# Two accumulator banks for the last sequence's second mixture, its halves normalised and stored apart, and a new order of issue

## The chip, the core and the metric

The kernel runs on one core of a Trainium2 chip. The metric is device time in microseconds (us) of one execution. Beside three timed executions there is one profiled execution, whose trace gives a start and a duration for every instruction.

The engines are called as the profile calls them: PE (matrix multiplication; PEld is its weight load, which runs beside it), DVE (vector engine), ACT (scalar engine), POOL (GpSimd) and SP, whose queue issues nearly all the transfers between the DRAM and the on-chip memory. PE writes into PSUM, which has 8 banks; one bank holds 128 x 512 numbers of 4 bytes.

## The reference

The input x is 8 sequences of 512 tokens of 128 features. Four stages follow one another, each of the form `x = layernorm(x + stage(x))`:

1. an encoder with linear attention (16 heads of 64, feature maps with a random projection, the keys' maximum over the whole data) and a feed-forward part of 512 hidden units,
2. a mixture of 8 experts of 64 hidden units, the two best per token ("first mixture"),
3. softmax attention with 16 heads and rotary positions,
4. a mixture of 8 experts of 176 hidden units, the two best per token, and one more expert that every token passes ("second mixture").

The change touches the fourth stage:

```
scores = softmax(xf @ gate_w.T)
_, idx = top_k(scores + gate_b, 2)
w      = take_along_axis(scores, idx)            # rw: (tokens, 8), zero elsewhere
h      = silu((xf @ w1 + b1) * (xf @ w3 + b3))   # for each expert
oe     = h @ w2 + b2
y      = einsum('te,ted->td', rw, oe)
z      = the shared expert, in the same form
x      = layernorm(x + y + z)
```

The layernorm has no gain and no bias here: `(x - mean) / sqrt(var + 1e-5)`, over 128 features.

## The kernel before

**Tiling.** P = 128, a sequence is NT = 4 tiles of 128 tokens. Every operation is first recorded as a "work" (one instruction, or a few that stay together). The function `issue` then issues the 4883 works in the order of a written-out list, `ORDER` (from L129). A second list, `BANK_OF`, gives every PSUM tile its bank, one digit each. Both lists were worked out by a planner beforehand. Each engine runs its own works in the order of the list; between engines there are only the semaphores that the data and the reuse of buffers and banks ask for. So the list decides what stands ahead of what in each engine's queue, and the stages of different sequences lie interleaved.

**The second mixture** is done in two ways. The tokens of sequences 0 to 5 are sorted by expert: POOL scatters them with indirect DMAs (L1664), the experts' tiles are worked through (weights fetched L1696, results stored L1703), and `combine` brings every sequence's tokens back: `xs`, the mixture's input with the shared expert, is loaded (L1853) into a buffer that all sequences share, eight indirect DMAs of POOL gather the results (L1672), DVE adds them with their gates (L1859), a layernorm follows, and SP stores the sequence (L1863). Sequences 6 and 7 go through `dense_mixture` (from L1497), with every expert for every token: at the end of the kernel the combines of sequences 4 and 5 lie beside the dense mixture of sequence 7, and that of 6 ends there as well.

**`dense_mixture`** first runs the router and turns its gates over by transposes (L1507, copied to the DRAM at L1510). The hidden units come in FC2 = 13 chunks of 128. One chunk takes
- a transfer that spreads the gates' rows over partitions (L1050),
- the products with W1 (L1521) and W3 (L1522) into a slot of two PSUM banks,
- ACT's copy of the first with its bias (L1524), after which the first bank is free,
- DVE's product of it with the second bank plus bias (L1526), after which the second bank is free,
- ACT's tanh (L1529), the multiplication with the gates' rows (L1531, on POOL for sequence 7 and on DVE for sequence 6), and DVE's last step of the silu (L1532),
- two chunks later, the product with W2 for the four token tiles (L1547), which adds into one bank `yp` over all the chunks.

PE does each float32 product in two passes, so a chunk's L1547 shows as x8.

After the last chunk DVE adds the residual to the 512 columns of `yp` (L1553), `layernorm` normalises the four tiles, and one transfer of 256 KB stores the sequence (L1555).

**`layernorm`** (L1024, with `moments`, L1010) takes four bn_stats (L1014) and four bn_aggr (L1016) on DVE, one addition of epsilon for the four tiles (L1018), one power of -1/2 on POOL (L1020), one multiplication on DVE for the shift (L1027) and four scalings on ACT (L1029). Its small buffers come from rings of two places for each name, shared by the layernorms of one lane, here "m"; the statistics' buffer has one place. So the power of a layernorm waits for the last scaling of the layernorm two before it, which reads the buffer that the power writes.

**The end.** After the last work SP and POOL read a flag (L1925) that would send the kernel into another form of the attention, and the program's end (L2019) drains every engine.

Of the kernel before, what the change touches and what calls it, by code (L numbers as in the profile page):

```python
# [31 lines left out]
ALU = mybir.AluOpType  # L32
# [3 lines left out]
P = 128  # L36
B, N, D = 8, 512, 128
# [92 lines left out]
    1319, 858, 983, 859, 1320, 984, 1313, 862, 985, 989, 860, 1321, 1316, 863, 861, 990, 864, 1001, 991, 865, 1317,  # L130
    866, 992, 867, 998, 868, 1318, 993, 1335, 869, 1334, 1322, 1000, 870, 1323, 628, 994, 880, 1324, 881, 1331,
    1325, 995, 1314, 999, 886, 1336, 1330, 883, 884, 1003, 1332, 1002, 1004, 887, 1005, 1350, 1333, 1351, 1006,
    882, 1010, 1009, 1337, 889, 1338, 1007, 1008, 890, 1352, 1011, 681, 888, 1370, 1012, 885, 1339, 1015, 1326,
    1020, 891, 1017, 1340, 1353, 1016, 1025, 1022, 892, 1021, 1327, 1018, 1030, 1013, 1341, 893, 1328, 1342, 1023,
    894, 1329, 1032, 895, 1027, 1019, 896, 1024, 898, 1026, 897, 899, 900, 901, 1346, 902, 904, 1343, 1031, 903,
    1371, 1028, 905, 1344, 906, 1345, 1372, 1029, 1300, 907, 1033, 911, 1354, 1014, 908, 1373, 909, 1034, 910,
    1046, 1133, 1035, 1355, 1134, 1039, 1037, 1347, 1038, 1036, 1041, 1042, 1043, 1040, 1050, 1135, 1044, 1049,
    1045, 1048, 1047, 1356, 1137, 1147, 1138, 1136, 1348, 1139, 1148, 1051, 1141, 1149, 1055, 1365, 1059, 1053,
    1151, 1374, 1057, 1366, 1054, 1052, 1375, 1061, 1367, 1058, 1056, 1062, 1060, 1063, 1711, 1357, 1140, 1064,
    1368, 1150, 1142, 1358, 1714, 1152, 1349, 1359, 1395, 1715, 1065, 1143, 1069, 1360, 1068, 1369, 1145, 1376,  # L140
    1067, 1066, 912, 1716, 682, 1070, 1396, 1399, 1400, 1153, 1071, 1144, 1361, 1091, 1240, 1095, 1146, 1717, 1093,
    1154, 1092, 1097, 1096, 1072, 1094, 1156, 1155, 1098, 1362, 1073, 1729, 1099, 1377, 1074, 1363, 1075, 1378,
    1718, 1076, 1364, 1730, 1157, 1077, 1078, 1158, 1385, 1079, 1082, 1386, 1080, 1083, 1174, 1719, 1081, 1379,
    1084, 1085, 1086, 1087, 1387, 1720, 1380, 1088, 1731, 1388, 1089, 1090, 1175, 1159, 1100, 1389, 1397, 1106,
    1160, 1721, 1381, 1101, 1161, 1162, 1382, 1383, 1712, 1722, 1163, 1165, 1103, 1164, 1107, 1384, 1166, 1723,
    1102, 1390, 1167, 1110, 1391, 1169, 1724, 1109, 1168, 1104, 1392, 2110, 1170, 1173, 1193, 1171, 1108, 1393,
    1172, 1179, 1394, 1111, 1176, 1398, 1402, 1733, 1105, 1178, 1401, 1403, 1732, 1404, 1112, 1177, 1405, 1113,
    1725, 1406, 1407, 1408, 1114, 1726, 1409, 1727, 1728, 1115, 1180, 1116, 1183, 1182, 1119, 1120, 1117, 1410,
    1123, 1181, 1118, 1124, 1122, 1734, 1121, 1125, 1126, 1411, 1184, 1735, 1187, 1412, 1185, 1414, 1186, 1736,
    1127, 1737, 1413, 1419, 1129, 1131, 1128, 1191, 1130, 1415, 1532, 1416, 1188, 1533, 1215, 1421, 1536, 1192,  # L150
    1420, 1546, 1189, 1422, 1417, 1534, 1537, 1547, 1538, 1418, 1190, 1535, 1540, 1429, 1548, 1424, 1539, 1431,
    1550, 1197, 1426, 1549, 1425, 1541, 1749, 1198, 1738, 1427, 1423, 1551, 1194, 1430, 1750, 1542, 1195, 1432,
    1543, 1199, 1751, 1428, 1200, 1552, 1196, 1545, 1445, 1745, 1201, 1744, 1713, 1752, 1433, 1214, 1746, 1739,
    1132, 1205, 1434, 1436, 1202, 1437, 1435, 1770, 1438, 1203, 1440, 1442, 1439, 1441, 1443, 1446, 1444, 1769,
    1447, 1204, 1740, 1553, 1771, 1206, 1209, 1207, 1772, 1555, 1753, 1208, 1554, 1450, 1544, 1448, 1451, 1210,
    1452, 1449, 1754, 1212, 1453, 1454, 1456, 1455, 1213, 1457, 1211, 1755, 1216, 1556, 1458, 1459, 1741, 1219,
    1461, 1460, 1218, 1462, 1742, 1463, 1747, 1217, 1557, 1464, 1756, 1757, 1468, 1466, 1465, 1220, 1748, 1467,
    1223, 1221, 1471, 1222, 1224, 1225, 1227, 1226, 1228, 1229, 1231, 1230, 1558, 1559, 1232, 1560, 1561, 1233,
    1562, 1794, 1564, 1743, 1563, 1565, 1472, 1234, 1566, 1473, 1568, 1235, 1798, 1236, 1567, 1569, 1237, 1758,
    1591, 1572, 1573, 1238, 1759, 1574, 1571, 1239, 1570, 1764, 1241, 1765, 1774, 1244, 1766, 1242, 1245, 1243,  # L160
    1773, 1257, 1248, 1258, 1760, 1575, 2111, 1578, 1592, 1576, 1249, 1246, 1247, 1250, 1775, 1251, 1577, 1259,
    1776, 1252, 1777, 1582, 1254, 1253, 1256, 1579, 1761, 1778, 1762, 2115, 1763, 1255, 1779, 2114, 1580, 1767,
    2116, 1581, 1639, 1784, 1768, 1785, 1780, 1583, 1786, 1586, 1781, 1782, 2112, 1585, 1783, 1787, 2510, 1584,
    1789, 1788, 1790, 1795, 1796, 2117, 1587, 1791, 1590, 1613, 1800, 1588, 1614, 1792, 1589, 1593, 1793, 2113,
    1596, 1797, 1595, 1799, 1801, 1802, 1803, 2118, 1594, 1804, 2119, 1597, 1806, 1808, 1601, 1805, 2120, 1807,
    1602, 1809, 2121, 1604, 2122, 1810, 1603, 1598, 1813, 1599, 2123, 1600, 1818, 1814, 2124, 1605, 1815, 1608,
    1820, 1819, 1823, 1607, 1816, 1811, 1817, 1606, 1821, 1812, 1828, 1824, 2125, 1825, 1822, 1298, 1830, 1609,
    1829, 1612, 1826, 1610, 1831, 1827, 1844, 1611, 1832, 2126, 2127, 1615, 1833, 2130, 1617, 1834, 1836, 1837,
    2129, 1835, 1616, 1840, 1839, 1838, 1846, 1618, 1847, 2131, 1841, 1842, 2128, 1843, 1622, 1851, 1619, 1845,
    2133, 1848, 1620, 1850, 1849, 1855, 2134, 1859, 1621, 1852, 1853, 1856, 2132, 2145, 2144, 2150, 1860, 2146,  # L170
    1854, 1857, 1858, 1861, 2149, 2135, 1862, 2154, 2151, 2136, 2137, 2153, 1626, 1863, 2138, 2155, 1623, 1866,
    2139, 2152, 2147, 1624, 1625, 1260, 2156, 1867, 2148, 1474, 1630, 2194, 1261, 2157, 1627, 2140, 1262, 1628,
    1864, 2141, 1299, 1263, 1629, 1264, 1265, 2158, 1266, 1267, 2198, 2142, 1268, 2143, 1469, 2159, 1301, 1631,
    1470, 2165, 1303, 2164, 1632, 1494, 2166, 1302, 1475, 2160, 1304, 1492, 1865, 1476, 1477, 1495, 1490, 1481,
    1478, 1633, 1479, 1491, 1496, 1480, 1482, 2167, 1493, 1634, 1483, 1497, 1484, 1635, 1498, 2169, 1485, 1486,
    1305, 1487, 2170, 1488, 1269, 2161, 1306, 1489, 2162, 2168, 1307, 2163, 1308, 1499, 1309, 1271, 1636, 1500,
    2171, 1310, 1699, 2174, 1503, 1272, 1637, 1270, 2173, 2195, 2172, 1638, 2511, 1502, 1273, 2184, 1640, 1506,
    2185, 1501, 1505, 2186, 1644, 1509, 2518, 1656, 1641, 1643, 1508, 1647, 1642, 2514, 1646, 1311, 1645, 1504,
    2187, 2175, 1870, 1648, 1274, 1507, 2515, 1649, 1510, 1650, 2516, 2199, 2188, 1511, 1657, 1275, 1871, 1651,
    1872, 1658, 1654, 1512, 1284, 2517, 1655, 1653, 1652, 1513, 2176, 1286, 2177, 1697, 1514, 2196, 2178, 1276,  # L180
    1515, 1659, 2179, 2519, 1517, 1660, 1518, 1521, 1519, 1278, 1516, 1698, 1522, 2520, 1523, 1520, 1279, 2521,
    1280, 1524, 2180, 1525, 1661, 1700, 2522, 1868, 1526, 2181, 1662, 1529, 1701, 2512, 1869, 3675, 2182, 1281,
    1530, 1282, 1889, 1702, 1527, 1528, 1283, 1663, 1285, 1895, 2200, 1664, 2523, 2038, 1531, 1890, 1931, 1703,
    1676, 1891, 1896, 1873, 1932, 2183, 1893, 2524, 1935, 1892, 1894, 1933, 1936, 1665, 1874, 1937, 1704, 1945,
    1939, 2529, 1875, 1934, 1946, 1876, 1897, 1705, 2525, 1706, 1707, 1880, 2534, 1938, 1948, 1708, 1940, 2190,
    1877, 1709, 2533, 1947, 1710, 2189, 3275, 1878, 1941, 2530, 1949, 2191, 1881, 1943, 1666, 2549, 1287, 2535,
    1879, 2531, 1942, 2192, 1882, 2532, 2098, 1944, 1950, 2550, 1883, 2513, 2193, 1884, 2197, 1885, 2536, 2201,
    1886, 1951, 2551, 1667, 2202, 1952, 1953, 1887, 2552, 2570, 1888, 2203, 1954, 1668, 2569, 1670, 2204, 1669,
    2208, 1671, 2206, 1288, 1672, 1292, 2205, 1673, 2207, 1899, 2537, 2209, 1898, 1294, 1956, 2210, 1674, 2526,
# [399 lines left out]
def kernel(ctx: ExitStack, tc: tile.TileContext, i: dict, out: bass.AP):  # L589
# [418 lines left out]

    def moments(lane, src, eps):

        st = tiny(lane, [P, NT, 6], "ln_st", 1)
        mv = tiny(lane, [P, NT, 2], "ln_mv")
        for t in range(NT):
            nc.vector.bn_stats(st[:, t, :], src[:, t, :])  # L1014
# [1008 lines left out]
```

## Time and profile before

| | us |
|---|---|
| median of three executions | 1111.16 |
| their range | 1108.29 to 1113.31 |
| profiled execution | 1104.42 |
| its span, first to last instruction | 1102.3 |
| PE, from its last matmul to the end of the span | 12.6 |

The profiled execution took 2.1 us more than its span and 6.7 us less than the median.

In the trace's lines the columns are: start and duration in us, engine, line of the code, operation, result <- operands (names of buffers), shape, and the count of instructions that the line puts together. A bracket holds the idle time of the engine just before them and the instruction that ended it. A line whose engine ends in q (SPq, POOLq) belongs to the engine's queue: issue of a transfer, waits, drains. In the table by stretches each row has, for each engine, its busy time with the count of instructions, then the clock granted to PE (1.00 is full speed), the share of the DMA engines' time, and the GB/s that they moved.

### The profile page before, as it was taken

How to read it: one execution, taken by the hardware profiler on the slowest of the kernel's cores; microseconds unless marked ns; L12 is line 12 of the kernel's file. 1: busy time of each engine (PE TensorE's matmuls, PEld its weight loads, DVE VectorE, ACT ScalarE, POOL GpSimd, SP SyncE). 2: the span in 40 equal slices, each digit the busy share in tenths (PEclk: the TensorE clock that was granted, in tenths of full speed). 3: DMA queues.
4: the chain of work that ended last, by engine and by line, in shares of the span. 5: the costliest groups of instructions: out<-in, count | busy, mean ns of one | idle time of the engine just before them, and what ended most of it. 6: DMA issues, size and time to landing. Idle time of an engine off the chain costs nothing. (4 is left out here: it accounts for less than half of the span.)

```text
span 1102.3 us, 16710 instructions
## 1 busy us (share of the span) xinstructions
PE 1027.1 (93%) x5689; PEld 579.1 (53%) x5689; DVE 816.3 (74%) x1929; ACT 714.8 (65%) x971; POOL 432.9 (39%) x386
## 2 busy tenths in 40 slices
PE   7999999998989999998999999999899988889995
PEld 4444444576564535565545545545587646453563
DVE  4865665788897756899776887877689865765875
ACT  3343545556646788756788687898666675778644
POOL 1222235123363523426763162554324402516363
PEclk9999999999999999999999999999999999889998
DMA  7027430353405132014332222331367866662542
GB/s 213 1 74 255 122 120 2 104 186 140 123 33 193 48 136 87 2 58 154 124 123 79 87 98 90 99 117 64 115 181 226 257 192 179 196 179 82 141 129 72
DMA packets 103372, 134.53 MB, mean 122 GB/s; under 512 B 19650, under 2 KB 60669, under 8 KB 103281
## 3 DMA queue, kind: packets, MB, share of 16 engines
q1 hardware_dynamic: 99905, 126.55, 36.5%
q0 software_dynamic: 3072, 6.30, 2.0%
q8 instruction: 47, 0.77, 0.3%
q10 hardware_dynamic: 304, 0.56, 0.1%
q14 instruction: 44, 0.36, 0.1%
HBM read 81.93 MB, written 54.43 MB: 124 GB/s over the span
## 5 line engine op out<-in xcount | busy, mean ns | idle before, releaser
L1338 ACT ACTIVATE scratch<-ps 128x1024 f32<-128x1024 f32 x256 | 248.7, 1027 | 63.6 <-PE ps L1332 54.9
L1344 PE MATMUL ps<-scratch,vv 128*32 128x512 f32 x1024 | 141.1, 608 | 1.9 <-ACT scratch L1338 1.0
L1089 POOL TENSOR_TENSOR scratch<-scratch 128x1024 f32<-128x1024 f32 x32 | 67.9, 2122 | 121.9 <-ACT scratch L1086 84.5
L1332 PE MATMUL ps<-qx,kx 32*128 32x512 f32 x512 | 72.6, 500 | 9.6 <-ACT scratch L1338 4.3
L826 ACT ACTIVATE scratch<-ps 128x1024 f32<-128x1024 f32 x32 | 32.3, 1020 | 64.5 <-PE ps L821 64.5
L1332 PEld LDWEIGHTS ps<-qx,kx 32*128 32x128 f32 x512 | 28.4, 183 | 85.0 <-ACT scratch L1338 31.2
L1113 PEld LDWEIGHTS ps<-scratch 128*128 128x128 f32 x512 | 60.6, 192 | 17.3 <-issue 7.4
L1065 PE MATMUL ps<-wq,scratch 128*128 128x512 f32 x128 | 65.8, 621 | 3.7 <-ACT scratch L1070 1.2
L1113 PE MATMUL ps<-scratch 128*128 128x128 f32 x512 | 64.1, 278 | 2.1 <-ACT scratch L1109 1.2
L1075 PE MATMUL ps<-wqf,scratch 128*128 128x512 f32 x128 | 64.2, 605 | 1.7 <-DMA scratch<-xT_d 1.5
L1664 POOL DMA_INDIRECT x_d<-scratch,slots x48 | 52.8, 1100 | 29.0 <-DVE m_base L1734 12.8
L860 PE MATMUL ps<-scratch,x_sb 128*128 128x512 f32 x128 | 62.6, 598 | 0.6 <-DVE scratch L837 0.5
L821 PE MATMUL ps<-scratch 128*128 128x512 f32 x128 | 62.7, 618 | 0.4 <-ACT scratch L813 0.4
L1672 POOL DMA_INDIRECT scratch<-x_d,slots x48 | 48.5, 1010 | 34.8 <-DVE m_ln_st L1014 13.5
L831 PE MATMUL ps<-scratch 128*128 128x512 f32 x128 | 60.9, 598 | 0.0
L1832 PE MATMUL ps<-scratch 128*128 128x256 f32 (+1 forms) x252 | 55.1, 357 | 5.3 <-DMA scratch<-w_d 4.5
L828 DVE TENSOR_REDUCE scratch<-scratch 128x16 f32<-128x1024 f32 x32 | 38.4, 1210 | 26.0 <-ACT scratch L826 26.0
L1020 POOL TENSOR_TENSOR f_ln_rs<-f_ln_ve,nhalf 128x4 f32<-128x4 f32 x24 | 26.4, 1100 | 76.0 <-DVE f_ln_ve L1018 74.5
L869 POOL TENSOR_TENSOR scratch<-scratch 128x1024 f32<-128x1024 f32 x7 | 16.5, 2357 | 94.5 <-ACT scratch L855 77.5
L1832 PEld LDWEIGHTS ps<-scratch 128*128 128x128 f32 x252 | 41.6, 199 | 14.6 <-ACT scratch L1338 4.3
L1344 PEld LDWEIGHTS ps<-scratch,vv 128*32 128x32 f32 x1024 | 22.6, 108 | 48.7 <-issue 37.2
L1070 ACT ACTIVATE scratch<-ps 128x1024 f32<-128x1024 f32 x32 | 32.8, 1023 | 22.4 <-PE ps L1065 19.8
(293 smaller groups left out, 2456.9 us busy)
## 6 DMA issues: line engine op xcount, KB each, us to landing
halves_d<-scratch SPq DMA_DIRECT2D x32, 512.0 KB
scratch<-w_d SPq DMA_DIRECT2D x42, 386.0 KB
x_d<-scratch SPq DMA_DIRECT2D x27, 512.0 KB
scratch<-g_d SPq DMA_DIRECT2D x68, 128.0 KB
kx<-halves_d SPq DMA_DIRECT2D x32, 256.0 KB
qx<-halves_d SPq DMA_DIRECT2D x32, 256.0 KB
scratch<-z_d SPq DMA_DIRECT2D x8, 520.0 KB
kvo_d<-scratch SPq DMA_DIRECT2D x8, 512.0 KB
```

Of the source, the lines that this page charges most:

```text
L821: nc.tensor.matmul(kp_ps[:, a, :], xT[:, t * P : (t + 1) * P], wk[:, a * 512 : (a + 1) * 512], start=True, stop=True,)
L831: nc.tensor.matmul(dp_ps[:, a, :], xT[:, t * P : (t + 1) * P], wkf[:, a * 512 : (a + 1) * 512], start=True, stop=True,)
L860: nc.tensor.matmul(xp_ps[:, a, :], x_of(b)[:, t, :], ek[:, t, a * 512 : (a + 1) * 512], start=(t == 0), stop=(t == NT - 1),)
L1065: nc.tensor.matmul(qp[:, a, :], xT[:, t * P : (t + 1) * P], wq[:, a * 512 : (a + 1) * 512], start=True, stop=True,)
L1075: nc.tensor.matmul(dp[:, a, :], xT[:, t * P : (t + 1) * P], wqf[:, a * 512 : (a + 1) * 512], start=True, stop=True,)
L1089: nc.gpsimd.tensor_tensor(pr, eq, zr[:, 0:HM], ALU.mult)
L1113: nc.tensor.matmul(at_ps[:, 0:D], qnT[:, c, :], kvo[:, c, :], start=(c == 0), stop=(c == 7))
L1332: nc.tensor.matmul(halves[g // 2][:, g % 2, :], kx[quarter, kt * P : (kt + 1) * P], qx[quarter, :], start=True, stop=True, tile_position=( ...
L1338: nc.scalar.activation(pr[:, 2 * a : 2 * a + 2], sc, AF.Exp, scale=1.0 / math.sqrt(HD2))
L1344: nc.tensor.matmul(av[32 * g : 32 * g + 32, :], vv[:, head_columns(4 * g + j, kt, j % 2)], pr[:, g, :], start=(j % 2 == 0 and kt == 0), st ...
L1664: inst = tc.nc.gpsimd.indirect_dma_start(out=rows_d, out_offset=bass.IndirectOffsetOnAxis(ap=slots_, axis=0), in_=tokens_, in_offset=None)
L1832: nc.tensor.matmul(to, w[:, c : c + P], xf, start=True, stop=True)
```

## The change

For sequence 7, the last, the second mixture gets two accumulator banks: the W2 products of token tiles 0 and 1 add into one and those of tiles 2 and 3 into the other, over all the chunks. The last chunk's products are issued as two groups, one for each bank. After them come, for each half, an addition of 256 columns, a layernorm of two tiles and a store of 128 KB. `moments` and `layernorm` take the count of tiles from their argument. Sequence 6, and the form that the flag would bring, keep one bank.

```
     def moments(lane, src, eps):
-        st = tiny(lane, [P, NT, 6], "ln_st", 1)
-        mv = tiny(lane, [P, NT, 2], "ln_mv")
-        for t in range(NT):
+        nt = src.shape[1]
+        st = tiny(lane, [P, NT, 6], "ln_st", 1)[:, 0:nt]
+        mv = tiny(lane, [P, NT, 2], "ln_mv")[:, 0:nt]
+        for t in range(nt):
             nc.vector.bn_stats(st[:, t, :], src[:, t, :])
...
-        nc.gpsimd.tensor_tensor(rs, ve, nhalf[:, 0:NT], ALU.pow)
+        rs = tiny(lane, [P, NT], "ln_rs")[:, 0:nt]
+        nc.gpsimd.tensor_tensor(rs, ve, nhalf[:, 0:nt], ALU.pow)
...
     def dense_mixture(xb, dst, gate=nc.vector):
...
-        yp = psb("yp", brief=False)
+        halves_of = [range(NT)] if gate is nc.vector else [range(0, NT // 2), range(NT // 2, NT)]
+        yps = [psb("yp", brief=False) for _ in halves_of]
...
-                with nc.together():
-                    for t in range(NT):
-                        nc.tensor.matmul(
-                            yp[:, t * D : (t + 1) * D], ahead[n - 2][:, t * P : (t + 1) * P],
-                            fw2[:, turns[n - 2], :],
-                            start=(n == 2 and t == 0), stop=(n == FC2 + 1 and t == NT - 1),
-                        )
+                parts = halves_of if n > FC2 else [range(NT)]
+                for ts in parts:
+                    with nc.together():
+                        for t in ts:
+                            nc.tensor.matmul(
+                                yps[t * len(yps) // NT][:, t * D : (t + 1) * D],
+                                ahead[n - 2][:, t * P : (t + 1) * P], fw2[:, turns[n - 2], :],
+                                start=(n == 2 and t % len(halves_of[0]) == 0),
+                                stop=(n == FC2 + 1 and (t + 1) % len(halves_of[0]) == 0),
+                            )
         res = tile2("m_res")
-        nc.vector.tensor_tensor(tok(res), tok(yp), xb, ALU.add)
-        layernorm("m", tok(res), tok(res), 1e-5)
-        nc.sync.dma_start(dst, tok(res))
+        for ts in parts:
+            some = slice(ts[0], ts[-1] + 1)
+            now = tok(res)[:, some]
+            nc.vector.tensor_tensor(now, tok(yps[ts[0] * len(yps) // NT])[:, some], xb[:, some], ALU.add)
+            layernorm("m", now, now, 1e-5)
+            nc.sync.dma_start(dst[:, some], now)
```

`ORDER` and `BANK_OF` are made anew, with 4889 works and one bank digit more. The six new works are a group of PE (the last chunk's products come as two groups of the same matmuls), three of DVE (a second addition L1553, a second L1018, a second L1027), a second power of POOL and a second store of SP; the counts of bn_stats, bn_aggr and ACT's scalings stay.

The first 943 works, up to about 281 us in the profiled execution, are in the same order as before. After that works have changed places with their neighbours on each engine:

| engine | works moved | of | largest shift, places |
|---|---|---|---|
| PE | 132 | 1227 | 6 |
| DVE | 536 | 1900 | 12 |
| ACT | 177 | 905 | 5 |
| POOL | 90 | 329 | 9 |
| SP | 166 | 501 | 13 |

33 of the 880 other PSUM tiles have another bank. For the last 45 us this means: the two accumulators hold banks 7 and 5 from the first W2 products of sequence 7 to their additions, and the two-bank slots of its chunks, which were the pairs from banks 0, 2 and 4 in turn, are the pairs from 0 and 2 alone.

Near the end the order is changed in these places. POOL issues all eight gathers of sequence 5 (L1672) ahead of the power of sequence 4's combine (L1020); before, seven stood ahead of it. In ACT's queue the first scaling of sequence 4's layernorm (L1029) stands ahead of a tanh (L1529) and of the bias copy of the next chunk (L1524). At the very end SP's stores come in the order: sequence 5, first half of 7, sequence 6, second half of 7. ACT's last scalings are those of sequence 6, 5 and 7 mixed, with the two pairs of sequence 7's halves last but for one of sequence 6 between them.

## The prediction on record

> **What bounds the kernel.** I read the page's shares first, then the table by stretches, then the timeline of the last 40 us.
>
> ```profile
> span 1102.3 us, 16710 instructions
> PE 1027.1 (93%) x5689; PEld 579.1 (53%) x5689; DVE 816.3 (74%) x1929; ACT 714.8 (65%) x971; POOL 432.9 (39%) x386
> ```
>
> PE is busy for 1027.1 of 1102.3 us. Of the 75.2 us in which it is not, 5.7 lie before the first matmul and 12.6 after the last (1088.58 + 1.16 = 1089.74 below), so some 57 us of idle time are spread over the whole. The change leaves PE's matmuls as they are, so it can gain in the 12.6 and 57 us only. By stretches:
>
> ```profile
> 1050.00:1090.00 40.00, 38.63 (x190) 24.56 (x189) 32.85 (x90) 18.00 (x32) 25.18 (x22) 1.00 0.36 102
> 1090.00:1102.30 12.30, 0.00 (x0) 0.00 (x0) 2.14 (x12) 4.59 (x12) 1.42 (x2) 0.67 0.25 70
> ```
>
> Where the accumulators are split, PE (first column after the length) is idle for 1.4 of 40 us. Then comes a tail without PE. In the timeline it reads:
>
> ```profile
> 1088.58 1.16 PE L1547 MATMUL ps<-scratch 128*128 128x128 f32 x8 [0.26 <-DVE scratch L1532]
> ...
> 1089.77 0.69 DVE L1553 TENSOR_TENSOR scratch<-ps,scratch 128x512 f32<-128x512 f32 x1 [0.15 <-PE ps L1547]
> ...
> 1092.42 1.01 POOL L1020 TENSOR_TENSOR m_ln_rs<-m_ln_ve,nhalf 128x4 f32<-128x4 f32 x1 [2.01 <-ACT scratch L1029]
> ...
> 1093.66 1.65 ACT L1029 ACTIVATE scratch<-scratch,m_ln_nm,m_ln_rs 128x128 f32<-128x128 f32 x4 [0.22 <-DVE m_ln_nm L1027]
> ...
> 1095.33 0.37 SPq L1555 DMA_DIRECT2D out_dram<-scratch  x1
> ```
>
> Addition, statistics, power, four scalings, store. The end itself is in the instructions of line 2019, by queue (durations in ns, least/median/most, then first and last start):
>
> ```profile
> L2019 POOLq DRAIN  x3: 40/107/7905, 1093.5 to 1102.0; - x3
> L2019 SPq DRAIN  x3: 7/7/13, 1099.5 to 1101.7; - x3
> ```
>
> SP, after the last store, drains at 1099.5. POOL's drain begins at 1093.5, right after its last power (1092.42 + 1.01), and takes 7.9 us, to 1101.4; the span ends 0.9 later. So **POOL's last power sets the end, 8.9 us after it; the last store has 1.9 us of slack** (1101.4 - 1099.5). Whether that drain is a fixed length after the power or waits for something else, this trace does not show; I keep both.
>
> **The change part by part.**
>
> *The end.* The last group of matmuls, 1.16 us, becomes two; the first half is complete some 0.5 earlier. Additions: 0.69 us for 512 columns, 0.34 us for 128; by the line between them 256 columns take 0.46, so the second half's addition ends at 1089.77 + 0.46 or, if it waits for the first, later by little. Statistics and scalings keep their counts (four bn_stats at 0.28, four bn_aggr, four L1029 at 0.4 to 0.48). Added on DVE's path are one L1018 and one L1027 (0.17 and 0.16), and a power on POOL. A power of two columns is not in the trace: it lies between 0.56 (eight rows, one column, L905) and 1.01 (four columns); I take 0.75. Both powers wait for rings: the first for the scalings of sequence 5, which have tiles 0 and 1 done by about 1091.5; it then runs to 1092.3. The second waits for its L1018 (about 1092.5, two statistics of the second half and the second small add behind the first half's) and ends between 1093.1 and 1093.7 instead of 1093.43. By POOL's drain the end moves by **-0.3 to +0.3; I take +0.1**, as two serial powers cost what the split wins. If the stores set the end instead, the last two scalings end at about 1094.95 instead of 1095.31 and the store is half as large: **-0.6 to -1.0**. Both ends are kept.
>
> At the trace's rows the halving of work per instruction is dear: 0.46 x 2 = 0.92 for 0.69 us of addition. [...]
>
> *The second bank* costs no instruction, but takes bank 5 from the slots of sequence 7's chunks: two slots instead of three. A slot is held from W1 to the end of L1526: two products of 0.86 us and a response, from W3's end to L1526's end, that was 0.85 to 1.9 us in this stretch but for one case. PE takes 2.6 us for a chunk, so two slots come round in 5.2 us and cover a response up to 2.6. The one case is here:
>
> ```profile
> 1062.78 1.05 POOL L1020 TENSOR_TENSOR m_ln_rs<-m_ln_ve,nhalf 128x4 f32<-128x4 f32 x1
> ...
> 1064.06 1.26 ACT L1029 ACTIVATE scratch<-scratch,m_ln_nm,m_ln_rs 128x128 f32<-128x128 f32 x3 [1.80 <-DVE m_ln_nm L1027]
> ...
> 1065.22 1.88 PE L1522 MATMUL ps<-scratch 128*128 128x512 f32 x4
> ...
> 1065.22 0.67 ACT L1524 ACTIVATE scratch<-ps,cols 128x512 f32<-128x512 f32 x1
> ...
> 1065.93 0.75 DVE L1526 SCALAR_TENSOR_TENSOR scratch<-ps,cols,scratch 128x512 f32<-128x512 f32 x1 [1.91 <-ACT scratch L1524]
> ```
>
> The bias copy waits behind three scalings of sequence 4's combine, which waited for its power. L1526 ends at 1066.68, 3.9 us after its matmuls. Before, the next products (second half of the x4 row, 1066.08) had a third slot. With two they go into this one: a stall of 1066.68 - 1066.08 = **0.6 us**. Besides, POOL now has one more gather (1.03 to 1.3 us with its issue) ahead of that power, and ACT a scaling ahead of a tanh and of this bias copy: the chain comes 1.3 us later, the stall is **1.9**. Against that, the planner's shifts may let the bias copy pass in time: 0. I take **1.3**, between the two stalls, as both moves are certain from the order and only their overlap with slack is not.
>
> *What then comes later.* Sequence 4's store waits for its scalings, and its buffer's next load for the store:
>
> ```profile
> 1066.82 0.41 SPq L1863 DMA_DIRECT2D out_dram<-scratch  x1
> ...
> 1070.58 0.34 SPq L1853 DMA_DIRECT2D scratch<-xs_d  x1
> ```
>
> The load came 3.8 us after the store and takes 4.5 us to land (the row of 1046.07). Later by 1.2 to 2.5, it delays the additions of sequence 5 (L1859, first at 1075.82), which stand in DVE's one queue ahead of L1526 and L1532 of two chunks; DVE is 82% busy here (32.85 of 40) and has little to give back. With that the last matmul comes up to **3.1** us later (1.9 and half of 2.5). If PE's slack of 1.4 us takes the delay up, nothing of it is left.
>
> *The rest of the order.* PE has 132 of 1227 works moved, by six places at most, DVE 536 of 1900. No instruction is added before 1050 us. The moves that looked dangerous are covered: a power moved behind six scatters (869) has them ready 10 us earlier, in a hole of POOL from 860 to 869; a result store (L1703) moved ahead by 13 places was ready long before. So I cost the rest at nothing. Its cover is those 57 us of idle time; about a tenth of PE's works have moved, and a tenth of 57 us is **6 us either way**, an estimate that serves as spread.
>
> **The sum.** End +0.1, stall and its consequences +1.3, rest 0: +1.4 on the profiled execution, 1104.4 -> 1105.8, and put on the median of the runs, 1111.16 -> **1112.6**. 0.5%, or 5.6 us, is about what a measurement of this kernel can tell from no change.
>
> **Rivals.**
> - *Two slots bind* (slower, 0.25). The stall at 1065 delays sequence 4's store, sequence 5's load and its additions, and each of the last chunks finds its slot held. For it: DVE at 82%, one queue for both. Against: all but one response fit into 2.6 us. It decides once two chunks in a row answer later than 2.6 us. +3.1, and with two more stalls of 1.9 up to +7: 1114.3 to 1118.2.
> - *The split does its work* (0.15). The drain follows the stores, or the early first half brings the second power forward, and the slots cost nothing: -1.0, with the gaps of 1.1 us before it closed as well -2.1: 1109 to 1110.2; with luck in the order down to 1105.
> - *It does not do what it says* (0.15). The stores' gain lies under POOL's drain, nothing is won at the end, and the reordering from 281 us on decides, by the spread of 6: 1105 or 1117. I lean to the slower side of it (0.09 to 0.06), since an engine that is 93% busy has less to win than to lose.
>
> **Chances and range.** The forecast gets 0.45 and stays within 0.5% (1105.6 to 1116.7), as do half of the first rival (0.12) and three quarters of the second (0.11): 0.68 together. Faster by more: 0.04 of the second and 0.06 of the third, 0.10. Slower by more: 0.13 of the first and 0.09 of the third, 0.22. The range goes from the third's lower end, 1105, to the first's upper end, 1118.2; it is wide because of the order, not of the split.
>
> **What would show it.** The forecast: in the changed trace a gap of PE of 0.6 to 2 us before an L1522 or L1521 near 1066, released by DVE's L1526; sequence 4's store about 1 us later; POOL's drain beginning at 1093 to 1095 and again near 8 us long; SP's drain well before its end. If the drain shrinks as the power moves, the end hangs on something else, and the second rival is right. Gaps of PE at every second chunk after 1070 would show the first. If the time before 1050 us differs by more than 2 us, the order has decided, and I was wrong to cost it at nothing. An added wait to see: the first power behind the scalings of sequence 5 (POOL's idle time before it released by ACT).

## The result and the profile after

| | us |
|---|---|
| median of seven executions before | 1111.16 (1107.31 to 1114.9) |
| median of seven executions after | 1121.22 (1116.92 to 1125.03) |
| profiled execution after, its span | 1120.62, 1118.9 |

The ratio is 1.0091, with a 95% interval of 1.0065 to 1.0117: slower by 10 us, above the upper end of the forecast range (1118.2).

The page of the profile after begins:

```profile
span 1118.9 us, 16724 instructions
PE 1032.4 (92%) x5689; PEld 585.3 (52%) x5689; DVE 813.1 (73%) x1932; ACT 714.3 (64%) x971; POOL 431.9 (39%) x387
```

PE's busy time is 5.3 us longer for the same 5689 matmuls (the mean granted clock of this execution was 0.981, and 0.987 before), and its idle time between the first and the last matmul is 68 us, where it was 57. The first 280 us agree within 0.1 us. The place of the predicted steps, the timeline of the last 40 us after (start, duration, engine, line; all lines have moved on by 2 to 10):

```profile
1078.54 1.04 POOL L1021 TENSOR_TENSOR m_ln_rs<-m_ln_ve,nhalf 128x4 f32<-128x4 f32 x1
...
1081.43 0.75 DVE L1530 SCALAR_TENSOR_TENSOR scratch<-ps,cols,scratch 128x512 f32<-128x512 f32 x1 [1.66 <-ACT scratch L1528]
...
1082.24 1.12 PE L1526 MATMUL ps<-scratch 128*128 128x512 f32 x2 [1.15 <-DVE scratch L1530]
...
1103.30 1.16 PE L1553 MATMUL ps<-scratch 128*128 128x128 f32 x8 [0.42 <-DVE scratch L1536]
...
1104.98 1.16 PE L1553 MATMUL ps<-scratch 128*128 128x128 f32 x8 [0.52 <-DVE scratch L1536]
```

This is the predicted stall: the W3 product waits 1.15 us for DVE's product to free one of the two slots, behind the power of sequence 4's combine. The last two groups wait 0.42 and 0.52 us, where only one waited 0.26. In the last 48 us before the last matmul's end PE is idle for 2.09 us after and 1.10 before. The end:

```profile
1105.90 0.42 DVE L1563 TENSOR_TENSOR scratch<-ps,scratch 128x256 f32<-128x256 f32 x1
...
1108.00 0.70 POOL L1021 TENSOR_TENSOR m_ln_rs<-m_ln_ve,nhalf 128x2 f32<-128x2 f32 x1 [1.24 <-DVE scratch L1563]
...
1109.00 0.69 POOL L1021 TENSOR_TENSOR m_ln_rs<-m_ln_ve,nhalf 128x2 f32<-128x2 f32 x1 [0.30 <-DVE m_ln_nm L1029]
```

Its drains, from the instructions of the program's end (ns; first and last start):

```profile
L2029 POOLq DRAIN  x3: 40/107/7905, 1109.8 to 1118.6; - x3
L2029 SPq DRAIN  x3: 7/7/13, 1115.3 to 1118.3; - x3
```

From PE's last matmul to the end it is 12.7 us after, 12.5 before (by the matmul's recorded end). So the last 60 us are as forecast, and some 15 us between the two profiled executions, 8 to 9 between the medians, came from 281 to 1040 us, where the forecast had put nothing. The largest single gap of PE there reads as follows in the timeline after:

```profile
1029.45 0.94 POOL L1682 DMA_INDIRECT scratch<-x_d,slots  x1 [0.30 <-issue]
...
1029.46 0.50 PE L1334 MATMUL ps<-qx,kx 32*128 32x512 f32 x4 [1.11 <-issue]
...
1034.90 1.94 ACT L1340 ACTIVATE scratch<-ps 128x1024 f32<-128x1024 f32 x2 [4.98 <-remote]
...
1036.89 0.80 PE L1334 MATMUL ps<-qx,kx 32*128 32x512 f32 x4 [4.85 <-ACT scratch L1340]
```

ACT's exponential reads the four products that PE issued at 1029.46 and that end by their model at 1029.96. ACT starts at 1034.90, released by no instruction that the trace knows ("remote"). In the trace's record of the semaphore, PE's own update, the signal that these products are done, is dated 4.9 us after their end. As that end is modelled, the trace can't tell a signal that came late from products that themselves ended late; in what follows "late" covers both. PE meanwhile issued what else it could, then waited for ACT. Comparing every update of PE's semaphore with the end of the last matmul ahead of it, I call a signal **late** when more than 0.3 us lie between. Up to 1070 us the sum of late stretches is 12.8 us in the trace before and 16.3 after. In both, every one over 0.5 us lies within 0.6 us of an issue of POOL's indirect DMAs; all the time so close to an issue is 14% of the span. ACT, DVE and POOL have no late signal before the program's end. Behind the stall the granted clock was halved for 6.8 us. In the table by stretches after (PE busy is the first number after the length, the clock the third from the end):

```profile
1020.00:1045.00 25.00, 18.16 (x119) 8.57 (x118) 10.88 (x31) 14.98 (x21) 8.79 (x9) 0.86 0.38 100
```

### The profile page after: what moved, and what is told of

Read it like the earlier page. It is cut to its first block, busy times and chain, and to the rows that moved or that the text cites. A ratio compares the mean times of both kernels' runs of the same rounds, so it can differ in the third digit from the quotient of the medians.

```text
span 1118.9 us, 16724 instructions
## 1 busy us (share of the span) xinstructions
PE 1032.4 (92%) x5689; PEld 585.3 (52%) x5689; DVE 813.1 (73%) x1932; ACT 714.3 (64%) x971; POOL 431.9 (39%) x387
## 5 line engine op out<-in xcount | busy, mean ns | idle before, releaser
L1340 ACT ACTIVATE scratch<-ps 128x1024 f32<-128x1024 f32 x256 | 249.2, 1027 | 74.1 <-PE ps L1334 54.5
L826 ACT ACTIVATE scratch<-ps 128x1024 f32<-128x1024 f32 x32 | 32.3, 1020 | 64.5 <-PE ps L821 64.5
L1674 POOL DMA_INDIRECT x_d<-scratch,slots x48 | 50.5, 1052 | 29.8 <-DVE m_base L1744 12.7
L1093 DVE TENSOR_REDUCE f_den<-scratch 128x16 f32<-128x1024 f32 x32 | 38.7, 1209 | 15.5 <-POOL scratch L1091 15.4
L1726 ACT ACTIVATE scratch<-scratch 128x512 f32<-128x512 f32 (+2 forms) x48 | 29.3, 614 | 30.9 <-DVE scratch L1722 16.6
```

The costliest lines, as they stand in the source:

```text
L1340: nc.scalar.activation(pr[:, 2 * a : 2 * a + 2], sc, AF.Exp, scale=1.0 / math.sqrt(HD2))
L1674: inst = tc.nc.gpsimd.indirect_dma_start(out=rows_d, out_offset=bass.IndirectOffsetOnAxis(ap=slots_, axis=0), in_=tokens_, in_offset=None)
```

## The experiments

Theory at first: the new order of the middle costs the time, the split what the prediction gave it. Rival: the second bank and the two slots cost it. In the edits, "order" stands for `ORDER` and `BANK_OF` together.

**1. The split with the old order, the new order without the split, and halves of it.** All four on one chip, on which before took 1094.44 us.

```
 split, old order       after.py:   order of before up to its 4600th work (1043 us), then the changed one
 new order, one bank    before.py:  changed order up to its 4600th work, then that of before
 first part             before.py:  changed order up to its 2867th work (700 us), then that of before
 second part            before.py:  changed order from the 2867th to the 4600th work
```

> The changed code with its two accumulators, its two slots and its own order for the last 60 us, but with the order and the banks of before up to about 1043 us. Theory 1 (the new order of the middle costs the time, the split only what the prediction gave it): +1 to +3 us, ratio 1.001 to 1.003. Theory 2 (the second bank and the two slots cost the time): +8 to +10 us, ratio 1.007 to 1.009.

> The code of before with one accumulator, one addition and one store, with the changed order and banks up to about 1043 us and the order of before for the last 60 us. Theory 1: +7 to +9 us, ratio 1.006 to 1.008. Theory 2: between -1.5 and +1.5 us.

> The code of before with the changed order and banks only up to about 700 us, the order of before from there on. Theory 1: by the lag of the two profiled executions at 700 us (3.7 us of 16) about a fourth of the loss, +2 to +4 us. Theory 2: between -1.5 and +1.5 us.

> The code of before with the changed order and banks only from about 700 to 1043 us. Theory 1: the rest of the loss, +5 to +7 us, so that this and the run with the first part add up to the run with both. Theory 2: between -1.5 and +1.5 us.

| | ratio to before | interval |
|---|---|---|
| split, old order | 1.0025 | 1.0005 to 1.0044 |
| new order to 1043 us, one bank | 0.9985 | 0.9965 to 1.0005 |
| first part | 0.9988 | 0.9966 to 1.0010 |
| second part | 0.9994 | 0.9970 to 1.0018 |

The split's +2.7 us fits both forecast and theory 1; the order costs nothing, against theory 1, which gave +7 to +9 us for it. Neither theory gives the 10 us. Part of the +2.7 us is probably not the split's own: in that trace PE also waits 1.86 us at the router's transposes of sequence 7 (L1509), just behind the place where the two orders join. There it waits 0.30 us in the trace before and not at all in that of the changed kernel. And before itself was 17 us quicker than in the first measurement. None of the four traces has a late signal.

**2. The changed kernel again, all of it but the split, and the last power left out.** A second such chip (before 1095.73).

```
 everything but the split   before.py with the changed order and banks throughout
```

```
-        nc.gpsimd.tensor_tensor(rs, ve, nhalf[:, 0:NT], ALU.pow)
+        nc.gpsimd.tensor_tensor(rs, ve, nhalf[:, 0:NT], ALU.pow) if power else nc.vector.tensor_copy(rs, ve)
...
-        layernorm("m", tok(res), tok(res), 1e-5)
+        layernorm("m", tok(res), tok(res), 1e-5, gate is nc.vector)
```

> The changed kernel itself, again, beside the kernel before. The parts measured so far (order of the middle -1.6 us, split with its end +2.7 us) add up to +1.1 us, not to the +10.1 us of the first measurement. If the parts simply add up, +0 to +3 us (ratio 1.000 to 1.003). If the parts hurt only together (order of the middle and the split), +8 to +12 us (1.007 to 1.011) wherever it is measured.

> The code of before, one accumulator, one addition and one store, but with the whole changed order and the changed banks, so also two slots instead of three for the last chunks and the changed queues of the last 60 us. If the slots and queues of the end make the loss of the split variant (+2.7 us), this stands 1 to 2 us above the run with the new order up to 1043 us (-1.6 us): -0.5 to +1 us, with a gap of PE of 0.6 to 1.9 us behind DVE's product of the chunk at the combine of sequence 4. If the halved normalisation makes it, -1.6 us and no such gap.

> The code and order of before; for the last sequence alone the power is left out and DVE copies the variance into its place, so its scalings use a wrong factor. If POOL's last power sets the end by its 7.9 us drain, POOL's last power is then the one of the layernorm before it, which ends 3.0 us earlier, and the time from the last matmul to the end of the span falls from 12.6 to some 9.5 to 10.0 us, the stores taking over. If the stores or something else set it, it falls by no more than the 0.9 us that the copy is shorter, to 11.7 or more, and POOL's drain changes its length.

The changed kernel: 0.9991 (0.9959 to 1.0022), so no loss. All but the split: 0.9983 (0.9955 to 1.0010), -1.9 us; with an interval from -4.9 to +1.1 us that can't decide between the two times expected of it, though the wait that was expected with the slots is there (0.90 us, below). The same place as above in this trace of the changed kernel:

```profile
1011.28 0.94 POOL L1682 DMA_INDIRECT scratch<-x_d,slots  x1 [0.31 <-issue]
...
1011.28 0.50 PE L1334 MATMUL ps<-qx,kx 32*128 32x512 f32 x4 [1.11 <-ACT scratch L1340]
...
1011.89 1.94 ACT L1340 ACTIVATE scratch<-ps 128x1024 f32<-128x1024 f32 x2
```

The same gather beside the same products; ACT starts 0.11 us after their end and does not wait. The stall of the two slots is there as well: 1.11 us in the changed kernel, 0.90 with one bank and the changed order, 1.22 in the split with the old order, and in none of the kernels with three slots. The end takes 13.4 us with the changed order and one bank, 12.7 with the split: the halves win back 0.7 us that their own order loses.

Without the last power the drains are:

```profile
L2019 POOLq DRAIN  x3: 40/107/7905, 1081.8 to 1091.7; - x3
L2019 SPq DRAIN  x3: 7/7/13, 1091.1 to 1091.4; - x3
```

POOL's drain has the same 7905 ns and begins behind what is now POOL's last power; it is over at 1089.7, and SP, with the stores, now comes last (1091.1). From the last matmul to the end it is 11.0 us instead of 12.5. I expected 9.5 to 10: the mechanism holds, the stores took 1 us more than I gave them.

**3. Where the loss comes back.** New theory A: the loss belongs to chips on which PE's signals come late. Rival B: it is in the order, and was missed by chance.

> The changed kernel a third time, to see on which chip it loses. In the first measurement (+10.1 us) the traces of both kernels hold signals of PE that come up to 4.9 us late, and before took 1111 us; on two other chips there were none, before took 1094 to 1096 us, and this kernel was not slower. Theory A (the loss belongs to a chip on which PE's signals come late): +8 to +12 us where before takes about 1111 us and the trace shows late signals, -3 to +3 us where before takes about 1095 us and it shows none. Theory B (the loss is in the order, and the second measurement missed it by chance): +5 us or more here, whatever the time of before.

> The code of before with the changed order and banks up to about 1043 us, again. Theory A: -2 to +1 us on a chip without late signals; on one with them most of the loss of the changed kernel, +6 to +10 us, as the late signals of its trace lie at 545 to 1035 us. Theory B: +4 us or more on any chip.

> The changed code with the order and banks of before up to about 1043 us, again. By the profiles its last 48 us hold 2 us of idle PE instead of 1, and the end is 0 to 0.2 us longer: +1 to +3 us on any chip, by both theories.

These three, unchanged from parts 1 and 2, fell on a third chip, where before took 1111.02 us:

| | ratio to before | interval |
|---|---|---|
| changed kernel | 1.0082 | 1.0051 to 1.0112 |
| new order to 1043 us, one bank | 1.0060 | 1.0029 to 1.0090 |
| split, old order | 1.0011 | 0.9982 to 1.0041 |

All three traces have late signals: 17.4, 19.6 and 15.8 us in sum. It went as theory A said, and B falls: the same kernels, 0.9985 and 0.9991 elsewhere, lose 6 and 9 us here, and most of it is the order's. At 546 us in the changed kernel's trace:

```profile
545.07 0.50 PE L1334 MATMUL ps<-qx,kx 32*128 32x512 f32 x4
...
545.12 0.96 POOL L1674 DMA_INDIRECT x_d<-scratch,slots  x1 [0.22 <-issue]
...
550.03 1.94 ACT L1340 ACTIVATE scratch<-ps 128x1024 f32<-128x1024 f32 x2 [5.02 <-remote]
```

Here POOL scatters, and the signal of the products of 545.07 is some 4 us late. In the first trace before, scatters lie at the same place, and ACT's exponential waited for nothing:

```profile
544.28 0.50 PE L1332 MATMUL ps<-qx,kx 32*128 32x512 f32 x4
...
545.25 1.96 ACT L1338 ACTIVATE scratch<-ps 128x1024 f32<-128x1024 f32 x2
...
545.56 1.48 POOL L1664 DMA_INDIRECT x_d<-scratch,slots  x1 [0.17 <-issue]
```

Part of the loss comes with the clock. The mean granted clock on this chip was 0.982 over the executions of before, 0.978 with the new order and 0.979 in the changed kernel. At the 0.8 us for each 0.001 that executions of before show (last section) that is an estimated 2 to 3 of the 6 and 9 us. Whether the stalls bring the clock down was not tested. The split in the old order again holds the wait behind the joint (1.73 us), so that PE idles 3.9 us in its last 48 us, not the 2 us expected.

**4. One stretch of the order, and no gathers.** A fourth chip, with late signals (before 1108.45).

```
 stretch   before.py:  changed order from the 4331st to the 4600th work (990 to 1043 us)
```

```
     def gather(group):
         def go(to, rows_d, slots_):
-            inst = tc.nc.gpsimd.indirect_dma_start(
-                out=to, out_offset=None, in_=rows_d, in_offset=bass.IndirectOffsetOnAxis(ap=slots_, axis=0)
-            )
-            apart("gather", group, inst, [("store", group)])
+            tc.nc.gpsimd.memset(to[:, 0:1], 0.0)
```

> The code of before with the changed order only between about 990 and 1043 us (works of 8 on PE, 23 on POOL, two PSUM tiles). Theory A (on a chip where PE's signals come late while POOL's indirect DMAs run, the new order puts more of them on PE's path): the traces from such a chip have one signal 4 to 5 us late behind the gathers at 1030 us with the new order and at most 1.3 us with the old one, so +3 to +6 us where before takes about 1111 us, and -1 to +1 us where it takes about 1095 us. Rival (the order costs by its queues on any chip, spread over all of it): +0.5 to +1.5 us anywhere, its share of the moved works.

> The changed kernel with the 48 gathers left out: POOL writes one column of the buffer instead, so sequences 0 to 5 add what lies there. Theory A: on a chip with late signals those after 900 us go (8 to 10 us of them in three traces, each followed by 1.7 us of a halved clock), so 9 to 15 us less than the changed kernel there, or -6 to 0 us against before; the late signals beside the scatters (545, 782, 875, 892 us) stay. On a chip without them -4 to 0 us against before, what the gathers' own waits cost. Rival (late signals have nothing to do with the indirect DMAs): the signals at 945, 978 and 1030 us stay late, and the time falls by no more than on other chips.

The stretch: 1.0002 (0.9980 to 1.0024). That expectation of theory A missed: with this stretch alone the signals beside the gathers at 1024 to 1028 us were 2.8 us late in sum, and nothing was lost. The changed kernel without gathers: 0.9907 (0.9888 to 0.9926), more than expected. 2.3 us of it lie at the end, which takes 10.4 us here, because POOL's drain is half as long:

```profile
L2029 POOLq DRAIN  x3: 40/107/3985, 1089.8 to 1096.2; - x3
```

With 96 indirect DMAs in the program this drain took 7905 ns, with the 48 scatters alone 3985 (also in the two runs of before without gathers, part 5), and without any (part 6) no drain of POOL at the end took over 82:

```profile
L2029 POOLq DRAIN  x3: 34/41/82, 1084.4 to 1090.3; - x3
```

That is some 82 ns for each indirect DMA, gather or scatter.

What theory A said of the signals came as said: after 900 us none is late; those beside the scatters at 545, 779 and 870 us stay (9.4 us in sum). So the late signals do hang on the indirect DMAs.

**5. The kernel before without gathers, and the new order to 990 us.** The first time these fell on a chip without late signals (before 1091.83) and could tell nothing apart there.

```
 no gathers          before.py with the edit of part 4
 new order to 990    before.py:  changed order up to its 4331st work
```

> The kernel before with the 48 gathers left out in the same way (POOL writes one column instead, sequences 0 to 5 add what lies there). The changed kernel without them stood at 0.991 of before on a chip with late signals. Theory A1 (the new order loses by the gathers' late signals): without gathers the two orders are alike there but for the split's 1 us, so 0.989 to 0.991 of before. Theory A2 (it loses by the scatters' late signals, at 545 to 892 us, or by its queues): the loss of 6 us stays between the two, so 0.983 to 0.986 of before. On a chip without late signals it tells them not apart: 0.994 to 1.000.

> The code of before with the changed order and banks up to about 990 us only. The stretch from 990 to 1043 us alone did not cost anything on a chip with late signals (1.0002). If the loss of the order lies ahead of it: +5 to +8 us on such a chip, ratio 1.0045 to 1.007. If it needs both stretches together: -1 to +3 us. On a chip without late signals -2 to +1 us by both.

Without gathers 0.9960 (0.9941 to 0.9980), with the new order to 990 us 0.9975 (0.9953 to 0.9996). Then, on a fifth chip, with late signals (before 1108.28), the same kernel without gathers and the first part of the order:

> The kernel before without gathers, again, for a chip with late signals; on one without it stood at 0.996 of before. If the new order loses by the gathers' late signals: 0.989 to 0.991 of before, as the changed kernel without gathers (0.991). If it loses by the scatters' late signals or by its queues: 0.983 to 0.986. On a chip without late signals 0.994 to 0.998 by both.

> The code of before with the changed order and banks only up to about 700 us, again, for a chip with late signals. There the changed order up to 1043 us cost 6.1 us, and its stretch from 990 us 0.2 us. If the loss lies at the scatters of 545 us (3.3 us late with the changed order in three of four traces, 0.3 to 0.4 us with the old one): +4 to +6 us, ratio 1.0035 to 1.0055. If it lies between 700 and 990 us: -1 to +1.5 us. On a chip without late signals -2 to +1 us by both.

Before without gathers: **0.9850** (0.9827 to 0.9873), so the gathers cost 16 us there and 4 where signals are on time, 1.9 us of each by the longer drain. The changed kernel without gathers stood at 0.9907: a difference of 0.0057, 6 us, is left without them. It is taken between two chips, its interval reaches from about 3 to 10 us, and it holds the split's own cost. By it the gathers' late signals are not the larger part of what the new order loses, but the interval leaves that open. The first part of the order, to 700 us: 1.0018 (1.0005 to 1.0032), +2.0 us, less than the expected 4 to 6 if the scatters at 545 us were all, and more than nothing.

**6. No indirect DMA at all**, in the changed kernel and in the one before, to tell the scatters' late signals from the order's queues.

```
     def scatter(group):
         def go(rows_d, tokens_, slots_):
             tc.nc.gpsimd.memset(between, 0.0)
-            inst = tc.nc.gpsimd.indirect_dma_start(
-                out=rows_d, out_offset=bass.IndirectOffsetOnAxis(ap=slots_, axis=0), in_=tokens_, in_offset=None
-            )
-            apart("scatter", group, inst)
```

> The changed kernel with all 96 indirect DMAs left out: no gathers (one column written by POOL instead) and no scatters (the experts fetch whatever lies in their buffers). On chips with late signals the changed kernel without gathers still stood 0.6% above before without gathers (0.991 to 0.985), and its trace has 9.4 us of late signals, all at scatters, to 4.4 us. If those late signals are the loss: no signal later than 0.5 us in either, and this one 0 to 2 us above the other (the split's own cost), so their ratios to before differ by no more than 0.002. If the order costs by its queues: 4 to 7 us stay between the two (0.004 to 0.006). On a chip without late signals 0 to 2 us by both.

> The kernel before with all 96 indirect DMAs left out in the same way. On a chip with late signals 0.975 to 0.985 of before, since the late signals of the scatters go too (4.4 us and the halved clock behind them); on one without 0.990 to 0.998. What tells the theories apart is its distance to the changed kernel of this call: 0 to 2 us, or 4 to 7 us.

0.9961 (0.9937 to 0.9984) and 0.9994 (0.9974 to 1.0014). This was a chip without late signals (before 1094.68): inconclusive for the question. And the expectation missed: 0 to 2 us were expected between the two here, and the changed kernel stood 5.0 us below the other (medians of 1090.19 and 1095.18 us; 3.6 us by the ratios), at a mean granted clock of 0.989 against 0.984. So the two kernels can stand nearly as far apart with no late signal at all.

**What stands and what is open.** On four measurements with late signals before took 1108 to 1111 us, on four without 1092 to 1096. The late stretches at five places where the orders differ, in us, each number one trace:

| beside | order of before there | changed order there |
|---|---|---|
| scatters at 545 us | 0.3, 0.4, 0, 0 | 1.2, 3.4, 3.3, 3.1, 3.7 |
| scatters at 698 to 710 us | 2.0, 3.0, 2.1, 0.7 | 0.8, 0.5, 0.8, 0.4, 0.4 |
| scatters at 870 to 893 us | 1.9, 2.1, 0.8, 1.7, 0.8 | 3.1, 2.0, 3.5, 3.3 |
| gathers at 931 to 981 us | 5.7, 5.7, 7.8, 8.0 | 3.7, 4.9, 5.4 |
| gathers at 1008 to 1034 us | 0, 1.6, 0 | 4.9, 4.0, 4.0, 2.8 |

The differences of the means are +2.8, -1.4, +1.5, -2.1 and +3.4, 4 us in sum, where the order lost 6.1. Over whole traces the late stretches tell the losing kernels hardly from the others: 16.3, 17.4 and 19.6 us where 6 to 10 us are lost, and 15.8, 16.2 and 15.9 in the split with the old order, the stretch alone and the first part, which lost 0 to 2. So how late the signals are in sum does not give the loss. If they cause it, it must be by where they fall, and that was not isolated: in the run of the stretch alone the last row's 2.8 us cost nothing, and without gathers some 6 us stayed. To 700 us the rows give 1.4 us against 2.0 measured. Between 700 and 990 us 4 us are lost by subtraction between chips, in a stretch that was not measured by itself on such a chip.

Shown is that the loss goes with the chips that have late signals: 1.0091 and 1.0082 for the changed kernel on two of them against 0.9991 on one without, 1.0060 for its order against 0.9985. That the late signals themselves are what it pays for, and through which waits, is argued; the clock has a part in it, and another difference of these chips is not ruled out.

## Why the prediction was wrong

**The step that failed** is "the rest of the order": "So I cost the rest at nothing. Its cover is those 57 us of idle time". It cost 6 us (1.0060) on a chip with late signals, such as that of the first measurement. The sign that the prediction named for this, more than 2 us of difference before 1050 us, came with some 15 us. My reading, which no run isolates, is that idle time of PE is no cover for PE's late signals, since it is there that the signal is waited for. Which waits carry the 6 us stays open. The spread of 6 either way had the right size by luck, as a tenth of PE's idle time has nothing to do with late signals or the clock; I took it as chance of either sign, put the case at 0.15 and its upper end at 1117. On chips without late signals the step was right: 0.9985 for the order, 0.9991 for the whole (+1.4 us, 1.0013, was forecast).

I had seen what should have warned me: the trace before has a stretch from 934 to 937 us in which PE and ACT stand still with their data ready. It is a late signal of 2.8 us beside a gather:

```profile
934.16 0.50 PE L1332 MATMUL ps<-qx,kx 32*128 32x512 f32 x2
...
934.71 0.96 POOL L1672 DMA_INDIRECT scratch<-x_d,slots  x1 [0.30 <-issue]
...
937.31 0.69 DVE L1351 COPY scratch<-ps 128x512 f32<-128x512 f32 x1 [3.82 <-remote]
...
938.05 1.45 PE L1332 MATMUL ps<-qx,kx 32*128 32x512 f32 x2 [3.39 <-DVE scratch L1351]
```

I costed moves by what waits for what, and did not ask what released that wait.

**The stall of two slots** was right in place, cause and size: 1.3 forecast, 1.11 to 1.24 measured in the five traces of the split with its gathers. Not foreseen were the two waits of the last groups (0.7 us more than before); they also came with one bank and the changed order (0.42 and 0.53), so they belong to the order and not to the halves. Two waits of before went, 0.30 us before 1060 and 0.54 at 1071, so that PE's idle time in the last 48 us grew by 1.0 in all. One reading was wrong: by the prediction's own figures two slots cover a response of 5.2 - 1.72 = 3.5 us, not of 2.6 (and its one case, 3.9, was to stall for 0.6). That made the first rival look likelier than it was.

**The cascade** did not come. Sequence 4's store is 0.4 us later against the last matmul, but the load of sequence 5's `xs` and its additions are 0.6 and 2.0 us earlier. The new order of the end had moved both forward, so the first rival did not come about, and slower came for another reason.

**The end** was right: +0.1 forecast, +0.2 measured; POOL's drain sets it, as the run without the last power shows (11.0 us from the last matmul instead of 12.5). The question that the prediction left open, whether the drain has a fixed length after the power, is answered in part 4: it starts behind the last power, and its length went with the number of indirect DMAs. The sizes inside: additions of 256 columns take 0.42 (0.46 taken), powers of two columns 0.69 and 0.70 (0.75 taken).

**The split by itself** is +2.7 us (1.0025) and +1.2 us (1.0011) in two measurements, whose intervals both hold the forecast +1.4. Both hold the wait of 1.7 to 1.9 us behind the joint of the two orders, which the changed kernel has not.

## What to carry to other kernels

When a change comes with a new order, cost the order as a term of its own, and look in the trace for engines that stand still with all data ready; here such stalls lay at certain places, and how long they were went with the order (beside the scatters at 545 us 0 to 0.4 us late with the order of before, 1.2 to 3.7 with the changed one, where signals came late at all). Before a difference of 1% is explained by the code, measure both kernels on more than one chip: here the same pair gave 1.009 and 0.999. Halving the last block won 0.7 us at the end in its own order and gave more than that back (a stall of 1.11 to 1.24 us) through the PSUM bank that it took from the slots.

## What the runs showed of the hardware

- In four measurements, on at least three chips, PE's semaphore updates came up to 4.9 us after the modelled end of the matmul, those over 0.7 us all within 0.6 us of an issue of POOL's indirect DMAs; in four others, on four other chips, none did, with the same kernels. Where they come late, the trace also lacks 4 to 5% of the engines' semaphore updates (2% without the gathers); elsewhere none. Why some chips do this, and whether it happens without a trace, is open.
- POOL's drain at the program's end took 7905 ns in every trace with 96 indirect DMAs, 3985 in the three with 48, and at most 82 in the two with none: some 82 ns for each indirect DMA. SP's took 7 to 13.
- While PE worked, the clock was halved in spells of 3.4 or 6.8 us (once 10.2): five in the trace before, nine in the one after. Among 35 executions of the kernel before on one chip the time fell by 0.8 us for each 0.001 of mean granted clock (correlation -0.83), which is most of its spread from 1090 to 1101 us.
